# A gated delta rule on one core: where the decays' projection and the triangles' products stand among the values' convolutions

## The chip, the cores and the metric

The kernel runs on one core of a Trainium2 chip. The metric is device time in microseconds (us) of one execution, given as the median of the runs shown. The program is one decoder layer, in 32-bit floats throughout; the change touches its first part, the delta-rule attention, and nothing else.

The engines are TensorE (PE in the profile; its weight loads are PEld), VectorE (DVE), ScalarE (ACT), GpSimd (POOL) and SyncE (SP, which issues transfers). Each works through a queue of its own in order.

## What is computed

The part that the change touches, cut to what matters (batch B = 4, T = 1024 tokens, H = 4 heads, keys of 64, values of 128):

```python
normed = (x - mu) * rsqrt(var + EPS) * ln_w + ln_b
q = causal_conv_silu(normed @ Wq, conv_q)      # four taps along the tokens
k = causal_conv_silu(normed @ Wk, conv_k)
v = causal_conv_silu(normed @ Wv, conv_v)
beta = sigmoid(normed @ Wb)
g = -exp(A_log) * softplus(normed @ Wa + dt_bias)
# q, k made unit length per head; then, token by token:
S = S * exp(g_t)
v_eff = (v_t - k_t @ S) * beta_t
S = S + outer(k_t, v_eff)
o_t = q_t @ S
# o normalised, gated with silu(normed @ Wg), projected with Wo, added to x; layernorm
```

After it come a cross attention, a mixture of experts and layernorms, which the change leaves alone.

## The kernel before

**Slabs.** The 1024 tokens are cut into NS = 8 slabs of 128 tokens, all four batches at once. The token-by-token recurrence is computed slab by slab in a block form: inside a slab the decays are summed with triangular matrices of ones, a triangular matrix per batch and head is inverted, and the state S is carried from slab to slab.

**Generators and rounds.** The work is written as Python generators, and `interleave` runs them in turns: in each round every generator advances to its next `yield`. What a generator writes between two yields is called a stage here. The turn decides the written order. A scheduler then fixes each engine's order when the program is built, with the written order as priority; the order seen in the trace is close to the written one, but not always the same.

**The loop.** For slab i there are two interleaves. The first one runs

- `prepares(i+1)`: two chains of `prepare`, each for two batches. Stages: a product on POOL (L494), the matmul `pe` (L500) with its Exp on ACT (L502) and a product on POOL (L504), then the matmuls `pk` (L514), then eight products on DVE in all per pair of batches that write `bp` (L525).
- `inverts(i)`: two `invert`s. Stages: transposes `pw` (L587) and their copies, matmuls `pl` of 32x32 (L597), `pu` (L613, L620) with copies into `tr` and `tt` (L623, L625), `pl` of 64x64 (L629), which reads `tr`, then `pu` of 64x64 (L634) with a copy (L636).
- one chain of `decays(i+2)`, `values(i)` and `cumulated(i+2)`, in this order.

`decays` has three stages of TensorE work: the transposes `pt` of each half of the normalised input (L335), each followed by an ACT copy into `nT` (L339), and then the projection `pb` (L352): eight matmuls with eight columns each, which read both copies. Behind it stand some twenty operations on 128x16 elements, nearly all on DVE, that make `beta` and `g` (L365 to L388).

`values` runs `convolve` for four chunks c and two halves j: eight stages. Each holds two matmuls (L287, four records in the trace, since a 32-bit matmul leaves two); after the yield come one ACT copy with a scale (L297) and three DVE multiply-adds (L299).

`cumulated` multiplies `g` with the triangular matrices `le`, `gt` and with `ones` (`pd`, L397), yields, and takes the Exp of the result on ACT (`ex`, L407); four DVE operations turn it into `el` and `qw` (L413 to L417).

Behind this interleave, `silus(i)` applies Silu to the four value tiles (L485). Each is told to be issued after all Exps collected in `exps`, that of `cumulated` among them, so that ACT's function table is changed once.

The second interleave runs `scans(i)` (the recurrence and the output; its first stage transposes keys and queries, `ptok` L647, and the values, `pv` L650; `qk` L653 is made of `ptok` and `qw`), `blocks(i+1)`, `project(i+2)` (the convolutions of keys and queries, by the same `convolve`) and `normed(i+3)`.

With no `i+2` (slabs 6 and 7) the chain is `values` alone. `decays(0)` and `decays(1)` run ahead of the loop, beside `normed(1)` and beside `cumulated(0)` and `project(0)`.

**Banks.** All these matmuls take their output from seven PSUM banks of one tag in turn.

Of the kernel before, what the change touches and what calls it, by code (L numbers as in the profile page):

```python
# [110 lines left out]
def kernel(ctx: ExitStack, tc: tile.TileContext, a: dict, out: bass.AP):  # L111
# [3 lines left out]
    def bc(ap, shape):  # L115
        return ap.to_broadcast(shape)
# [5 lines left out]
    def bank(name, tag="bank", bufs=None):  # L122
        kw = {} if bufs is None else {"bufs": bufs}
        return ps_pool[0].tile([P, 512], F32, tag=tag, name=name, **kw)
# [96 lines left out]
    def interleave(*gens):  # L221

        gens = list(gens)
        while gens:
            for g in list(gens):
                if next(g, gens) is gens:
                    gens.remove(g)
# [53 lines left out]
    def convolve(dst, c, nT):  # L281

        w0 = C_CONV + c * KCONV
        for j in range(2):
            pp = bank("pp")
            for kc in range(KC):
                mm(  # L287
                    pp[:, 0 : 2 * (HALO + P)],
                    lhsT=wqkv[:, kc, c * P : (c + 1) * P],
                    rhs=nT[:, kc, 2 * j : 2 * j + 2, :].rearrange("p b t -> p (b t)"),  # L290
                    start=kc == 0,
                    stop=kc == KC - 1,
                )
            yield
            pre = pp[:, 0 : 2 * (HALO + P)].rearrange("p (b t) -> p b t", b=2)
            ch = dst[:, 2 * j : 2 * j + 2, :]
            nc.scalar.activation(ch, pre[:, :, 0:P], AF.Identity, scale=cols[:, w0 : w0 + 1])  # L297
            for n in range(1, KCONV):
                nc.vector.scalar_tensor_tensor(  # L299
                    ch, pre[:, :, n : n + P], cols[:, w0 + n : w0 + n + 1], ch, ALU.mult, ALU.add  # L300
                )
# [21 lines left out]
    def decays(i, made):  # L323

        nrm = made["nrm"]
        nT = slab.tile([P, KC, B, HALO + P], F32, tag="nT", name="nT")
        if i:
            nc.gpsimd.tensor_copy(nT[:, :, :, 0:HALO], before[-1][:, :, :, P:])
        else:
            nc.gpsimd.memset(nT[:, :, :, 0:HALO], 0.0)  # L330
        before.append(nT)
        for c in range(KC):
            pt = bank("pt")
            for b in range(B):
                nc.tensor.transpose(  # L335
                    pt[:, b * P : (b + 1) * P], nrm[b][:, c * P : (c + 1) * P], ident
                )
            yield
            nc.scalar.activation(  # L339
                nT[:, c, :, HALO:],  # L340
                pt.rearrange("p (b t) -> p b t", b=B),
                AF.Identity,
                scale=cols[:, C_LNW + c : C_LNW + c + 1],
                bias=cols[:, C_LNB + c : C_LNB + c + 1],
            )


        pb = bank("pb")
        pba = pb[:, 0 : B * 2 * H].rearrange("p (b n) -> p b n", b=B)
        for b in range(B):  # L350
            for kc in range(KC):
                mm(  # L352
                    pba[:, b, :],
                    lhsT=nT[:, kc, b, HALO:],
                    rhs=wba[:, kc, :],
                    start=kc == 0,
                    stop=kc == KC - 1,
                )
        yield

        def small(name):
            return slab.tile([P, B, H], F32, tag=name, name=name)

        beta, za, u, s, s2, p, g = (small(n) for n in ("beta", "za", "u", "s", "s2", "p", "g"))
        nc.scalar.activation(beta, pba[:, :, 0:H], AF.Exp, scale=-1.0)  # L365
        nc.vector.tensor_tensor(
            za,
            pba[:, :, H : 2 * H],
            bc(rows[:, R_DT : R_DT + H].unsqueeze(1), [P, B, H]),
            ALU.add,  # L370
        )
        nc.vector.tensor_scalar_add(beta, beta, 1.0)
        nc.vector.reciprocal(beta, beta)

        nc.vector.scalar_tensor_tensor(u, za, -1.0, za, ALU.mult, ALU.max)
        nc.scalar.activation(u, u, AF.Exp, scale=-1.0)
        nc.vector.tensor_scalar_add(s, u, 2.0)
        nc.vector.reciprocal(s, s)
        nc.vector.tensor_tensor(s, s, u, ALU.mult)
        nc.vector.tensor_tensor(s2, s, s, ALU.mult)  # L380
        nc.vector.tensor_scalar_mul(p, s2, 1.0 / 17)
        for k in (15, 13, 11, 9, 7, 5, 3):
            nc.vector.scalar_tensor_tensor(p, p, 1.0 / k, s2, ALU.add, ALU.mult)
        nc.vector.scalar_tensor_tensor(p, p, 1.0, s, ALU.add, ALU.mult)
        nc.vector.tensor_scalar_max(za, za, 0.0)
        nc.vector.scalar_tensor_tensor(g, p, 2.0, za, ALU.mult, ALU.add)
        nc.vector.tensor_tensor(g, g, bc(nega.unsqueeze(1), [P, B, H]), ALU.mult)
        nc.vector.tensor_scalar_max(g, g, -1e30)  # L388

        made.update(nT=nT, g=g, beta=beta)  # L390
# [83 lines left out]
    def values(made):  # L474
        made["v"] = v = [slab.tile([P, B, P], F32, tag=f"v{c}", name="v", bufs=1) for c in range(H)]
        for c in range(H):
            yield from convolve(v[c], NQK + c, made["nT"])
    def silus(made):

        with ExitStack() as behind:  # L480
            for e in exps:
                behind.enter_context(tc.issue_after(e.ins))
            exps.clear()
            for v in made["v"]:
                nc.scalar.activation(v, v, AF.Silu)  # L485
# [4 lines left out]
    def prepare(i, b, made):  # L490

        g, kq = made["g"], made["kq"]
        ee = work("ee", [P, H, 2, P])
        nc.gpsimd.tensor_tensor(  # L494
            ee[:, :, 1, :], bc(le.unsqueeze(1), [P, H, P]), bc(g[:, b, :].unsqueeze(2), [P, H, P]), ALU.mult
        )
        yield

        pe = bank("pe")
        mm(pe, lhsT=gt, rhs=ee[:, :, 1, :], start=True, stop=True)  # L500
        exps.append(
            nc.scalar.activation(ee[:, :, 0, :], pe.rearrange("p (h t) -> p h t", h=H), AF.Exp)  # L502
        )
        nc.gpsimd.tensor_tensor(  # L504
            ee[:, :, 1, :], ee[:, :, 0, :], bc(nge.unsqueeze(1), [P, H, P]), ALU.mult
        )
        yield

        bp = made["bp"]
        pks = [bank("pk") for par in range(2)]  # L510
        for r in range(2):
            for par, pk in enumerate(pks):
                h0 = slice(par * HK, (par + 1) * HK)
                mm(  # L514
                    pk[:, r * 2 * P : (r + 1) * 2 * P],
                    lhsT=kq[r][h0, 0, b, :],
                    rhs=kq[r][h0, :, b, :],
                    start=True,
                    stop=True,
                )  # L520
        yield
        for par, pk in enumerate(pks):
            for r in range(2):
                h = 2 * r + par
                nc.vector.scalar_tensor_tensor(  # L525
                    bp[:, :, b * H + h],
                    pk[:, r * 2 * P : (r + 1) * 2 * P].rearrange("p (n t) -> p n t", n=2),
                    made["nb"][:, b, h : h + 1],
                    ee[:, h],
                    ALU.mult,  # L530
                    ALU.mult,
                )
# [268 lines left out]
    made = [{} for _ in range(NS)]  # L801
# [6 lines left out]
    def prepares(i):  # L808
        made[i]["bp"] = slab.tile([P, 2, B * H, P], F32, tag="bp", name="bp", bufs=2)
        made[i]["tt"] = tts[i % 2]  # L810
        gens = [prepare(i, b, made[i]) for b in range(B)]
        return [chain(*gens[n::2]) for n in range(2)]

    def inverts(i):
        return [invert(b, made[i]) for b in range(0, B, 2)]

    def scans(i):
        return [
            chain(scan(i, b, made[i]), scan(i, b + 1, made[i])) for b in range(0, B, 2)
        ]  # L820
# [4 lines left out]
    def some(f, i, *args):  # L825
        return [f(*args, made[i])] if i < NS else []
# [5 lines left out]
    interleave(blocks(0, made[0]), *some(project, 1, 1))  # L832
    for i in range(NS):
        ahead = prepares(i + 1) if i + 1 < NS else []
        interleave(
            *ahead,
            *inverts(i),
            chain(*some(decays, i + 2, i + 2), values(made[i]), *some(cumulated, i + 2)),
        )
        silus(made[i])  # L840
        if i + 1 < NS:
            interleave(
                *scans(i), *some(blocks, i + 1, i + 1), *some(project, i + 2, i + 2), *some(normed, i + 3, i + 3)
            )
# [816 lines left out]
```

## Time and profile before

| what | us |
|---|---|
| median of three runs (1768.39, 1771.73, 1775.53) | 1771.73 |
| the profiled execution, device time | 1777.84 |
| its span, first to last instruction | 1776.1 |
| PE busy / DVE busy / ACT busy / POOL busy in the span | 1589.0 / 1177.7 / 935.8 / 565.8 |
| mean granted TensorE clock | 0.945 |

The delta rule takes some 800 us of the span. A slab begins with its transposes `pw`; these start at 108.5, 200.4, 290.9, 384.7, 476.8, 568.9, 659.6 and 737.1 us, so a slab takes these times (each window is one slab):

| slab | us | PE busy | DVE busy | ACT busy |
|---|---|---|---|---|
| 0 | 91.9 | 87.41 | 66.36 | 50.60 |
| 1 | 90.5 | 84.77 | 70.10 | 51.93 |
| 2 | 93.8 | 86.95 | 69.27 | 51.84 |
| 3 | 92.1 | 85.97 | 69.28 | 51.87 |
| 4 | 92.1 | 86.08 | 69.21 | 51.89 |
| 5 | 90.7 | 86.05 | 67.98 | 49.98 |
| 6 | 77.5 | 70.96 | 51.80 | 39.17 |

How to read the lines below: in the timeline each line has start and length in us, the engine, the line of the kernel, the operation, output and inputs, shape and number; a bracket tells how long the engine was idle before it and what ended the idle time. In the table of windows each pair is busy time and number of instructions, and PEclk is the granted clock as a share of full speed.

### The profile page before, as it was taken

How to read it: one execution, taken by the hardware profiler on the slowest of the kernel's cores; microseconds unless marked ns; L12 is line 12 of the kernel's file. 1: busy time of each engine (PE TensorE's matmuls, PEld its weight loads, DVE VectorE, ACT ScalarE, POOL GpSimd, SP SyncE). 2: the span in 40 equal slices, each digit the busy share in tenths (PEclk: the TensorE clock that was granted, in tenths of full speed). 3: DMA queues.
4: the chain of work that ended last, by engine and by line, in shares of the span. 5: the costliest groups of instructions: out<-in, count | busy, mean ns of one | idle time of the engine just before them, and what ended most of it. 6: DMA issues, size and time to landing. Idle time of an engine off the chain costs nothing. (4 is left out here: it accounts for less than half of the span.)

```text
span 1776.1 us, 28454 instructions
## 1 busy us (share of the span) xinstructions
PE 1589.0 (89%) x9524; PEld 1152.4 (65%) x9524; DVE 1177.7 (66%) x3557; ACT 935.8 (53%) x2214; POOL 565.8 (32%) x486
## 2 busy tenths in 40 slices
PE   4658999999989998985889999999989999999991
PEld 3246777676767766762657777887765666666660
DVE  4658686877777776735456888888865655555554
ACT  3425555555556454551278888888743333333333
POOL 2311312121212112014045666666733322222222
PEclk9869999898989898998999999999999999999995
DMA  4010101010101010103050011111263322332226
GB/s 142 18 19 22 39 19 43 19 43 19 43 19 30 19 31 19 25 31 132 0 190 13 22 46 43 37 49 37 94 216 67 69 45 46 46 48 46 45 33 199
DMA packets 119023, 94.20 MB, mean 53 GB/s; under 512 B 56939, under 2 KB 108639, under 8 KB 118367
## 3 DMA queue, kind: packets, MB, share of 16 engines
q1 hardware_dynamic: 100127, 69.14, 13.6%
q0 software_dynamic: 13296, 17.83, 6.0%
q10 hardware_dynamic: 5456, 5.41, 0.9%
q8 instruction: 78, 1.28, 0.3%
q14 instruction: 66, 0.54, 0.1%
HBM read 55.46 MB, written 36.90 MB: 52 GB/s over the span
## 5 line engine op out<-in xcount | busy, mean ns | idle before, releaser
L1536 POOL DMA_INDIRECT xd<-my,mrow x71 | 110.6, 1557 | 294.4 <-ACT my L1535 268.7
L1105 ACT ACTIVATE sc<-sc,ntop,rq 128x77 f32<-128x77 f32 x512 | 182.4, 448 | 5.2 <-DVE ntop L1100 4.6
L1136 PE MATMUL pxo<-ball,aT 128*128 128x256 f32 (+1 forms) x640 | 151.4, 384 | 0.8 <-DVE xs L1147 0.8
L287 PE MATMUL pp<-nT,wqkv 128*128 128x262 f32 x512 | 149.1, 430 | 0.2 <-PE pu L620 0.2
L1066 POOL TENSOR_TENSOR rq<-rq,nhalf 128x8 f32<-128x8 f32 x64 | 106.8, 1669 | 129.2 <-DVE rq L1065 128.1
L1487 PE MATMUL pgt<-wall,mxT 128*128 x284 | 134.6, 596 | 0.5 <-ACT mxT L1420 0.5
L1487 PE MATMUL pup<-wall,mxT 128*128 x284 | 134.4, 596 | 0.0
L1514 PE MATMUL pdn<-wdn,mhT 128*128 x568 | 134.2, 379 | 0.0
L759 POOL TENSOR_TENSOR so<-so,nhalf 128x4 f32<-128x4 f32 x32 | 32.6, 1018 | 312.3 <-DVE so L758 312.3
L1136 PEld LDWEIGHTS pxo<-ball,aT 128*128 128x128 f32 (+1 forms) x640 | 118.0, 192 | 15.1 <-DVE xs L1147 1.4
L1049 PE MATMUL pq<-wdn,xT 128*128 128x512 f32 x256 | 120.6, 594 | 1.5 <-ACT qsq L1059 1.0
L299 DVE SCALAR_TENSOR_TENSOR kq<-pp,cols,kq 128x256 f32<-128x256 f32 x192 | 88.3, 478 | 38.9 <-ACT kq L297 36.3
L287 PEld LDWEIGHTS pp<-nT,wqkv 128*128 128x128 f32 x512 | 99.6, 209 | 21.8 <-issue 3.3
L1514 PEld LDWEIGHTS pdn<-wdn,mhT 128*128 128x128 f32 x568 | 102.5, 190 | 11.0
L1495 DVE TENSOR_TENSOR sge<-pgt,ball 128x512 f32<-128x512 f32 x71 | 49.1, 692 | 85.3 <-PE pgt L1487 84.4
L1496 ACT ACTIVATE sge<-sge 128x512 f32<-128x512 f32 x71 | 44.7, 630 | 111.8 <-DVE sge L1495 111.8
L1487 PEld LDWEIGHTS pup<-wall,mxT 128*128 128x128 f32 x284 | 54.5, 192 | 69.0 <-issue 69.0
L1497 DVE TENSOR_TENSOR pup<-pup,ball 128x512 f32<-128x512 f32 x71 | 49.7, 699 | 69.8 <-PE pup L1487 69.7
L1114 POOL TENSOR_TENSOR sc<-sc,den 128x616 f32<-128x616 f32 x64 | 78.2, 1221 | 55.0 <-DVE den L1113 41.0
L1535 ACT ACTIVATE my<-my,mw 128x256 f32<-128x256 f32 x71 | 36.1, 508 | 106.3 <-DVE my L1534 106.3
L299 DVE SCALAR_TENSOR_TENSOR v<-pp,cols,v 128x256 f32<-128x256 f32 x192 | 81.6, 476 | 13.9 <-ACT v L297 13.2
L1085 PE MATMUL psc<-wdn,qT 128*128 128x154 f32 x512 | 78.7, 295 | 7.2 <-ACT qT L1077 7.2
(313 smaller groups left out, 3693.9 us busy)
## 6 DMA issues: line engine op xcount, KB each, us to landing
mx<-xg SPq DMA_DIRECT2D x71, 130.0 KB, 2.1
xs<-xd SPq DMA_DIRECT2D x12, 512.0 KB, 9.5
xi<-in_x SPq DMA_DIRECT2D x8, 512.0 KB, 5.1
am<-ab SPq DMA_DIRECT2D x16, 256.0 KB, 3.7
xd<-kd SPq DMA_DIRECT2D x32, 128.0 KB, 1.7
wall<-in_L_ffn_gate_w SPq DMA_DIRECT2D x8, 512.0 KB, 9.6
wall<-in_L_ffn_up_w SPq DMA_DIRECT2D x8, 512.0 KB, 8.6
xd<-xs SPq DMA_DIRECT2D x8, 512.0 KB, 4.8
```

The lines of the kernel that those rows point to most:

```text
L287: mm(pp[:, 0 : 2 * (HALO + P)], lhsT=wqkv[:, kc, c * P : (c + 1) * P], rhs=nT[:, kc, 2 * j : 2 * j + 2, :].rearrange("p b t -> p (b t)"), ...
L299: nc.vector.scalar_tensor_tensor(ch, pre[:, :, n : n + P], cols[:, w0 + n : w0 + n + 1], ch, ALU.mult, ALU.add)
L1049: mm(pq, lhsT=t["xT"][:, kc, :], rhs=xwq[:, kc, c0 : c0 + HH * XD], start=kc == 0, stop=kc == KC - 1,)
L1066: nc.gpsimd.tensor_tensor(rq, rq, nhalf[:, :HH], ALU.pow)
L1085: mm(ps[:, c * 2 * SC : (c + 1) * 2 * SC], lhsT=qT[:, 2 * g + c, :], rhs=kbd[:, b, half * XC // 2 + 2 * g + c, :], start=True, stop=True,)
L1105: nc.scalar.activation(sc[:, h], sc[:, h], AF.Exp, scale=t["rq"][:, h : h + 1], bias=t["ntop"][:, h : h + 1])
L1114: nc.gpsimd.tensor_tensor(sc, sc, bc(den.unsqueeze(2), [P, HH, SC]), ALU.mult)
L1136: mm(px[:, 0:D], lhsT=aT[:w, c, :], rhs=vo[:w, b, half * NV + c, :], start=half == 0 and c == 0, stop=half == 1 and c == NV - 1,)
L1487: mm(ps, lhsT=t["xT"][:, c, :], rhs=wall[:, bass.ds(e * EW + off + c * FF, FF)], start=c == 0, stop=c == KC - 1,)
L1497: nc.vector.tensor_tensor(pu, pu, ball[:, bass.ds(e * FF + B_U, FF)], ALU.add)
L1514: mm(px[:, 0:D], lhsT=t["hT"][:, f, :], rhs=wdn[:, bass.ds(e * EV + f * D, D)], start=f == 0, stop=f == FC - 1,)
L1536: nc.gpsimd.indirect_dma_start(out=xd, out_offset=bass.IndirectOffsetOnAxis(ap=row, axis=0), in_=y, in_offset=None, compute_op=ALU.add,)
```

## The change

Two edits. In `decays`, a `yield` is put between the second copy into `nT` and the projection `pb`, so that `pb`, the small operations behind it and all that follows in the chain move one round back. In the loop, the chain takes five stages of `values`, then `cumulated`, then the other three stages, instead of all eight and then `cumulated`. `islice(vals, 5)` stops right after the fifth yield: the matmuls of the fifth convolution are written, its copy and multiply-adds are written after `cumulated`.

```diff
@@ decays @@
                 bias=cols[:, C_LNB + c : C_LNB + c + 1],
             )
 
+        yield
 
         pb = bank("pb")
@@ the loop @@
     for i in range(NS):
         ahead = prepares(i + 1) if i + 1 < NS else []
+        vals = values(made[i])
         interleave(
             *ahead,
             *inverts(i),
-            chain(*some(decays, i + 2, i + 2), values(made[i]), *some(cumulated, i + 2)),
+            chain(*some(decays, i + 2, i + 2), islice(vals, 5), *some(cumulated, i + 2), vals),
         )
```

By rounds, the chain's TensorE work stands so, for slabs 0 to 5:

| round | before | after |
|---|---|---|
| 1, 2 | `pt` | `pt` |
| 3 | `pb` | nothing |
| 4 | convolution 0 | `pb` |
| 5 | 1 | convolution 0 |
| 6 to 9 | 2 to 5 | 1 to 4 |
| 10 | 6 | `pd` |
| 11 | 7 | convolution 5 |
| 12 | `pd` | 6 |
| 13 | | 7 |

The other generators of that interleave keep their rounds: `pl` of 64x64 stands in round 4, `pe` of the second pair of batches and `pu` of 64x64 in round 5, `pk` in round 6.

## The prediction

> **What bounds the kernel now.** I read the page's head first, then the windows of one slab, then the timeline around the changed lines in slabs 0 and 1.
>
> ```profile
> span 1776.1 us, 28454 instructions
> PE 1589.0 (89%) x9524; PEld 1152.4 (65%) x9524; DVE 1177.7 (66%) x3557; ACT 935.8 (53%) x2214; POOL 565.8 (32%) x486
> ```
>
> TensorE is busy in 89% of the span. But the change lives in a stretch of some 25 us in each slab, and there the mean says little. The windows of slab 1 (its `pw` starts at 200.4):
>
> ```profile
> 212.00:214.00 2.00, 1.61 (x27) 1.61 (x28) 1.75 (x8) 0.74 (x2) 1.27 (x2) 1.00 0.00 0
> 214.00:216.00 2.00, 2.00 (x12) 1.68 (x10) 0.91 (x5) 1.37 (x4) 0.78 (x1) 0.50 0.00 0
> 224.00:226.00 2.00, 2.00 (x9) 1.49 (x10) 2.00 (x8) 0.57 (x2) 0.00 (x0) 1.00 0.00 0
> 230.00:232.00 2.00, 0.77 (x6) 0.46 (x5) 2.00 (x6) 1.87 (x4) 0.00 (x0) 1.00 0.69 97
> 236.00:238.00 2.00, 1.46 (x12) 0.82 (x12) 1.96 (x4) 1.58 (x8) 0.00 (x0) 0.97 0.00 0
> ```
>
> The third pair is DVE. From 224 to 238 it is full, while PE (first pair) falls to 0.77 of 2 us at 230: the values' multiply-adds are DVE's backlog, and PE waits behind them. Later in the slab, from 250 on, PE is full. So two things count: when DVE's backlog ends, and what PE and ACT do until then.
>
> **Where the triangles' products hurt today.** Slab 0, end of the first interleave:
>
> ```profile
> 137.02 7.13 DVE L299 SCALAR_TENSOR_TENSOR v<-pp,cols,v 128x256 f32<-128x256 f32 x18
> 139.21 0.74 PE L397 MATMUL pd<-g,sq 128*128 128x16 f32 x6
> 139.98 0.21 ACT L407 ACTIVATE ex<-pd 128x48 f32<-128x48 f32 x1
> 140.21 1.28 ACT L485 ACT_TABLE_LOAD   x1
> 141.51 1.67 ACT L485 ACTIVATE v<-v 128x512 f32<-128x512 f32 x3
> 142.19 0.41 PE L650 MATMUL pv<-sq,v 128*128 128x128 f32 x1 [1.76 <-ACT v L485]
> 146.10 0.47 ACT L297 ACTIVATE kq<-pp,cols 128x256 f32<-128x256 f32 x1 [2.92 <-PE pp L287]
> 146.47 0.62 ACT L485 ACTIVATE v<-v 128x512 f32<-128x512 f32 x1
> ```
>
> `pd` comes behind all eight convolutions, the Exp behind `pd`, the table load behind the Exp, the first Silu behind the load: PE idles 1.76 us for it. The fourth value tile is complete on DVE at 144.15 (137.02 + 7.13), yet its Silu starts at 146.47: ahead of it in ACT's queue stands the copy of the next keys' convolution, whose matmuls on PE were late. The same tail in slab 1:
>
> ```profile
> 234.73 0.47 ACT L297 ACTIVATE kq<-pp,cols 128x256 f32<-128x256 f32 x1 [0.97 <-PE pp L287]
> 235.48 0.63 ACT L485 ACTIVATE v<-v 128x512 f32<-128x512 f32 x1 [0.27 <-DVE v L299]
> ```
>
> Here the key copy comes before DVE is done (235.44), and the last Silu follows at once. Reading the other slabs so: 0, 2, 3 and 4 lose 2.3 us between DVE's end and the last Silu, 1 and 5 lose 0.1 or less. And slabs 0, 2, 3, 4 last 91.9, 93.8, 92.1, 92.1 us, slabs 1 and 5 only 90.5 and 90.7.
>
> **Edit two, `pd` after five convolutions.** Nothing is added: six records of `pd` (0.74 us), one Exp (0.21), four DVE operations (235.36 to 235.95, 0.6 us). No transfer and no POOL work belongs to it; SP's and POOL's queues stay as they are.
> - Is `g` there? In slab 1 the last operation on `g` ends at 224.9. Convolutions 2 to 7 are 24 records in 5.57 us (slab 0), 0.23 each, so from 223.83 the twelve records of 2, 3 and 4 end at 226.6. `g` has 1.7 us to spare. Should PE wait in `pd`, convolutions 5 to 7 are behind it, and DVE waits for those: but ACT's last value copy ends at 230.1 and its multiply-adds begin at 234.0 (235.44 less three of 0.476), so 3.9 us of stall are covered.
> - The Exp then stands three convolutions earlier, 12 x 0.23 = 2.8 us. The load of 1.28 us and the first Silus fall between the value copies, where ACT now idles 0.41 us at a time; ACT's lead of 3.9 us takes the 1.28 + 2 x 0.62 = 2.5 us. [...]
> - Gain, first term: PE does `ptok`, `pv` and the key matmuls earlier, the key copy is ahead of DVE's end in every slab, and slabs 0, 2, 3 and 4 go as 1 and 5 do: 91.9 + 93.8 + 92.1 + 92.1 = 369.9, less 4 x 90.6 = 362.4, is **7.5 us**. The bounds are 0 (the orders stay) and 9.2 (4 x 2.3, the whole delay).
> - Gain, second term: the 1.76 us of idle PE goes in all six slabs. It is worth something only if PE moves work of its full part into it: one more round of key matmuls, 4 x 0.23 = 0.93 us, 5.6 in six slabs. If no bank is free it is worth 0. Between the two I take the middle, **2.8 us**, for banks are freed by DVE at one in 1.43 us just then.
> - The four small DVE operations move ahead of the last nine multiply-adds. DVE's sum is the same and `qk` behind them ends when it did: 0. If the last Silu sets the end instead, it is 0.6 later, 3.6 us in six slabs.
>
> **Edit one, the yield.** It removes and adds no instruction.
>
> ```profile
> 209.21 1.95 PE L352 MATMUL pb<-wba,nT 128*128 128x8 f32 x16
> 211.92 0.75 DVE L623 COPY tr<-pu 32x256 f32<-32x256 f32 x2
> 212.39 2.38 PE L629 MATMUL pl<-tr,bp 64*64 64x64 f32 x32 [1.23 <-DVE tr L623]
> 214.70 2.11 PE L287 MATMUL pp<-nT,wqkv 128*128 128x262 f32 x4
> 216.61 2.28 PE L500 MATMUL pe<-ee,sq 128*128 128x512 f32 x4
> ```
>
> `pb` starts at 209.21; its second copy ended at 208.4, so in the loop there is hardly a wait to remove. What stands next, `pl`, needs `tr`, which DVE copies only at 211.92, behind eight `bp` products. `pb` fills this hole. I take it that the order stays, as `pb` has its inputs 4 us before `pl` has: **0**. The other end is the first rival.
> - Convolution 0 goes behind `pe` and `pu`. PE's sum is equal. On DVE, three multiply-adds (1.43 us) come later, out of a stretch with gaps (0.91 of 2 us busy at 214); in return `pe` comes up to 2.1 us earlier, and with it eight `bp` products (3.2 us). I take **0**; the ends are 1.43 x 6 = 8.6 us lost and 2.1 x 6 = 12.6 gained, neither likely in full.
> - Ahead of the loop, `pb` of slab 1 moves behind one more key convolution (0.93 us) in a stretch where PE is full: 0, between -1 and +1.
>
> **The sum.** 7.5 + 2.8 = 10.3 us off. The profiled execution (1777.84, of which 1.7 outside its span) would become 1767.5; it is 6.1 above the median, and I apply the difference to the median: 1771.73 - 10.3 = **1761.4 us**. Its own range, with both gains at their ends and some loss on DVE, is 1756 to 1767.
>
> **Rivals.**
> - *`pb` lands behind `pl`* (slower). Then PE idles from 209.2 to 212.4, 3.2 us instead of 1.23, and `pb`'s 1.95 us follows `pl` uncovered: all behind it, DVE's backlog too, ends 1.95 later, 6 x 1.95 = 11.7. `g` comes later than convolution 4, so the first edit's gain goes too: **1783.4**. For it: the written order now says so. Against it: `pl` is not ready when PE is free. It decides as soon as the records of L352 follow those of L629. On the clock: after the 1.23 us gap the granted clock is already 0.50 at 214. [...]
> - *DVE gives it back* (no change). Convolution 0's multiply-adds all fall into the full stretch: +8.6, with the gain of 10.3: **1770.0**. For it: DVE is full from 224 to 238. Against it: the earlier `bp`.
> - *It doesn't do what it says* (no change). The decays' small operations, a round later, bring `g` after convolution 4; `pd` goes on behind the last convolution, and the Exp is as late as now: **1771.7**. For it: the 1.7 us to spare are less than the 1.95 of `pb`. Against it: without convolution 0 between them the small operations run closer together.
>
> **How the numbers follow.** Forecast 0.50, `pb` behind `pl` 0.28, DVE gives back 0.12, no effect 0.10. A measurement here tells about 0.5% (8.9 us) from no change: faster is below 1762.9, slower above 1780.6. Of the forecast four fifths lie below 1762.9: faster 0.40. The rest of it, 0.10, and the two cases without change give 0.32 for the same; slower 0.28. The range must reach to the slower case and take the larger gains: 1752 (both gains at their ends, 14.8, and a part of `pe`'s) to 1785.
>
> **What would show it.** Right: L352 still ahead of L629 on PE; `pd` between the value convolutions; the table load of L485 before the last value copy of L297; the 1.76 us before `pv` gone; the last Silu within 0.3 us of DVE's end in all slabs; slabs 0, 2, 3 and 4 at 90.6 or less. Wrong: L352 behind L629 with 3 us idle before it, an idle PE before `pd` released by `g`, or DVE's value products ending later in the slab than 35.0 to 37.6 us after its `pw`.

## The result, and the profile after

| kernel | median us | before, same chip | ratio to before, 95% interval |
|---|---|---|---|
| changed | 1796.86 | 1773.15 | 1.0128 [1.01, 1.0155] |

The change makes the kernel slower by 23.7 us, 1.3%. The forecast was 1761.4 in a range of 1752 to 1785: wrong in its sign, and the range misses by 12 us. The head of the page of the changed kernel:

```profile
span 1798.4 us, 28454 instructions
PE 1608.0 (89%) x9524; PEld 1167.0 (65%) x9524; DVE 1181.6 (66%) x3557; ACT 933.2 (52%) x2214; POOL 565.4 (31%) x486
```

The same instructions, a span 22.3 us longer, and 19 us more of busy TensorE: the matmuls themselves took longer. Slabs 0 to 5, from one first `pw` to the next, now take 94.5, 95.2, 96.0, 95.5, 95.9 and 93.4 us: 570.5 together, against 551.1 before. Slab 6, without these edits, adds 1.5 and the start 1.0.

The timeline of slab 1 (`pw` at 204.0) where the yield was put (lines past the yield are one higher now: L353 is `pb`, L624 the copy into `tr`, L630 the 64x64 `pl`):

```profile
215.62 0.75 DVE L624 COPY tr<-pu 32x256 f32<-32x256 f32 x2
216.18 3.64 PE L630 MATMUL pl<-tr,bp 64*64 64x64 f32 x32 [3.29 <-DVE tr L624]
219.75 3.58 PE L353 MATMUL pb<-wba,nT 128*128 128x8 f32 x16
223.18 3.76 PE L501 MATMUL pe<-ee,sq 128*128 128x512 f32 x4
226.87 3.67 PE L635 MATMUL pu<-tt,wt 64*64 64x64 f32 x32
230.48 2.11 PE L287 MATMUL pp<-nT,wqkv 128*128 128x262 f32 x4
232.52 3.67 PE L515 MATMUL pk<-kq 64*128 64x256 f32 x16
```

`pb` now stands behind `pl`. TensorE waits 3.29 us for `tr`, where it waited 1.23, and the same matmuls take half as long again or more: `pl` 3.64 instead of 2.38 us, `pb` 3.58 instead of 1.95, `pu` 3.67 instead of 2.07, `pk` 3.67 instead of 2.0. Why, the windows of the same slab show (window, length, then PE, PEld, DVE, ACT, POOL busy, then the granted clock):

```profile
214.00:216.00 2.00, 0.00 (x0) 0.00 (x0) 1.97 (x7) 0.00 (x0) 1.31 (x2) 0.87 0.00 0
216.00:218.00 2.00, 1.82 (x17) 1.85 (x18) 1.27 (x5) 0.36 (x1) 1.78 (x2) 0.50 0.03 8
222.00:224.00 2.00, 2.00 (x8) 1.66 (x8) 0.42 (x4) 0.63 (x2) 0.00 (x0) 0.50 0.00 0
228.00:230.00 2.00, 2.00 (x21) 2.00 (x21) 1.93 (x5) 1.04 (x3) 0.92 (x1) 0.50 0.00 0
234.00:236.00 2.00, 2.00 (x12) 1.33 (x8) 1.51 (x7) 0.00 (x0) 0.00 (x0) 0.51 0.00 0
236.00:238.00 2.00, 2.00 (x11) 1.63 (x10) 2.00 (x7) 0.47 (x1) 0.85 (x1) 1.00 0.00 0
```

The granted clock is 0.50 from 216 to 236, twenty microseconds. Before, it was 0.50 at 214 and back at 1.00 by 218, as the two windows of before that follow the prediction's row for 214 show:

```profile
216.00:218.00 2.00, 2.00 (x5) 1.07 (x5) 0.82 (x4) 0.96 (x2) 0.00 (x0) 0.65 0.00 0
218.00:220.00 2.00, 2.00 (x23) 1.24 (x22) 2.00 (x4) 1.94 (x4) 1.26 (x2) 1.00 0.00 0
```

With the change, VectorE (third pair) starves in that stretch: 0.42 of 2 us at 222.

The end of the first interleave in slab 0, whose lines of before the prediction showed:

```profile
144.38 0.74 PE L398 MATMUL pd<-g,sq 128*128 128x16 f32 x6
144.97 2.90 PE L287 MATMUL pp<-nT,wqkv 128*128 128x262 f32 x12
145.38 1.28 ACT L486 ACT_TABLE_LOAD   x1
146.68 0.63 ACT L486 ACTIVATE v<-v 128x512 f32<-128x512 f32 x1
146.79 5.31 DVE L299 SCALAR_TENSOR_TENSOR v<-pp,cols,v 128x256 f32<-128x256 f32 x13
148.14 0.27 PE L651 MATMUL pv<-sq,v 128*128 128x128 f32 x1
151.06 0.47 ACT L297 ACTIVATE kq<-pp,cols 128x256 f32<-128x256 f32 x1 [0.64 <-PE pp L287]
152.14 0.63 ACT L486 ACTIVATE v<-v 128x512 f32<-128x512 f32 x1 [0.60 <-DVE v L299]
```

Here the second edit did what was forecast: `pd` has three convolutions behind it, the table load stands among the value copies, `pv` no longer waits 1.76 us, the key copy is early and the last Silu follows VectorE's end (152.10) at once. But all of it comes late: VectorE's last value product ends 42.6 us after `pw`, instead of 35.6.

So each slab has a front that grew and a tail that shrank. For slabs 1 to 4, from `pw` to the end of VectorE's value products: 43.8 us on average (43.3 to 44.2) instead of 36.1 (35.1 to 37.6), 7.7 longer; from there to the next `pw`: 51.9 instead of 56.1, 4.2 shorter.

### The profile page after: what moved, and what is told of

Read it like the earlier page. It is cut to its first block, busy times and chain, and to the rows that moved or that the text cites. A ratio compares the mean times of both kernels' runs of the same rounds, so it can differ in the third digit from the quotient of the medians.

```text
span 1798.4 us, 28454 instructions
## 1 busy us (share of the span) xinstructions
PE 1608.0 (89%) x9524; PEld 1167.0 (65%) x9524; DVE 1181.6 (66%) x3557; ACT 933.2 (52%) x2214; POOL 565.4 (31%) x486
## 5 line engine op out<-in xcount | busy, mean ns | idle before, releaser
L287 PE MATMUL pp<-nT,wqkv 128*128 128x262 f32 x512 | 140.1, 412 | 0.3 <-PE pu L621 0.2
L1138 PEld LDWEIGHTS pxo<-ball,aT 128*128 128x128 f32 (+1 forms) x640 | 118.0, 192 | 15.1 <-DVE xs L1149 1.4
L287 PEld LDWEIGHTS pp<-nT,wqkv 128*128 128x128 f32 x512 | 95.5, 199 | 20.7 <-issue 3.1
L299 DVE SCALAR_TENSOR_TENSOR v<-pp,cols,v 128x256 f32<-128x256 f32 x192 | 81.2, 478 | 13.2 <-ACT v L297 12.5
```

What stands on the lines that cost most here:

```text
L287: mm(pp[:, 0 : 2 * (HALO + P)], lhsT=wqkv[:, kc, c * P : (c + 1) * P], rhs=nT[:, kc, 2 * j : 2 * j + 2, :].rearrange("p b t -> p (b t)"), ...
L299: nc.vector.scalar_tensor_tensor(ch, pre[:, :, n : n + P], cols[:, w0 + n : w0 + n + 1], ch, ALU.mult, ALU.add)
L1138: mm(px[:, 0:D], lhsT=aT[:w, c, :], rhs=vo[:w, b, half * NV + c, :], start=half == 0 and c == 0, stop=half == 1 and c == NV - 1,)
```

## The experiments

Ten kernels were run, each beside the kernel before. Theory A was formed from the trace above: the yield costs, by the order of `pb` and by the clock, and the second edit gains.

| kernel | median us | its before | ratio, 95% interval |
|---|---|---|---|
| second edit alone (`pd` behind five) | 1763.31 | 1774.89 | 0.9929 [0.9908, 0.9949] |
| first edit alone (the yield) | 1799.21 | 1774.89 | 1.0129 [1.0091, 1.0166] |
| both, the yield behind `pb` | 1763.37 | 1774.89 | 0.9927 [0.9896, 0.9958] |
| changed, wide filler | 1781.39 | 1774.89 | 1.0023 [1.0, 1.0046] |
| second edit alone, wide filler | 1762.49 | 1774.07 | 0.9929 [0.991, 0.9947] |
| changed, narrow filler | 1795.97 | 1774.07 | 1.0114 [1.0088, 1.0139] |
| `pd` behind three | 1774.31 | 1774.07 | 1.0004 [0.9988, 1.002] |
| `pd` behind four | 1774.99 | 1775.06 | 1.0002 [0.9988, 1.0016] |
| `pd` behind six | 1759.39 | 1775.06 | 0.9924 [0.99, 0.9947] |
| a convolution ahead of `pb` | 1767.20 | 1775.06 | 0.9963 [0.995, 0.9976] |

**The two edits apart.** The second edit alone, against the changed kernel, as are the edits below where nothing else is said:

```diff
-        yield
```

> The second edit alone: pd behind five convolutions, no yield in decays. Theory A (the yield costs, since pb no longer fills the hole ahead of the 64x64 pl and TensorE then runs at half clock for some 19 us instead of 8; the second edit gains): faster than before, 1758 to 1768 us, the 64x64 pl starting 12 us after its slab's pw as before, values' last multiply-add 35 to 37 us after it. Theory B (the loss comes from pd itself, which cuts the convolutions and puts the table load among the value copies): slower than before, 1780 us or more.

The first edit alone, here against the kernel before:

```diff
+        yield
 
         pb = bank("pb")
```

> The first edit alone: the yield in decays, pd behind all eight convolutions. Theory A: slower than the changed kernel, since the second edit's gain is missing too, 1797 to 1815 us; the hole before the 64x64 pl is 3.6 us and the granted clock 0.50 until about 31 us after pw. Theory B: near before, 1765 to 1780 us.

Theory A holds in both, theory B in neither: the second edit alone gains 11.6 us, the yield alone loses 24.3. Of theory A's clock, down until some 31 us after `pw` with the yield alone, slabs 0, 1 and 4 show it (30.5 to 32.2 us); in slabs 2, 3 and 5 it is back at 19.8 to 23.6 us. The tail of slab 3 with the second edit alone (`pw` at 379.7):

```profile
408.81 1.28 ACT L485 ACT_TABLE_LOAD   x1
411.56 0.27 PE L650 MATMUL pv<-sq,v 128*128 128x128 f32 x1
414.87 0.47 ACT L297 ACTIVATE kq<-pp,cols 128x256 f32<-128x256 f32 x1 [0.64 <-PE pp L287]
415.94 0.63 ACT L485 ACTIVATE v<-v 128x512 f32<-128x512 f32 x1 [0.60 <-DVE v L299]
```

No wait before the first `pv`, and the last Silu right behind VectorE (415.91), 36.2 us after `pw` instead of 38.2. Slabs 0 to 5 take 88.5, 89.2, 89.1, 88.4, 88.4 and 86.0 us. But it is not only this wait that counts. TensorE's waits from 26 to 50 us after `pw` (those above 0.25 us, added up) shrink only from 3.7 to 2.8 us a slab. The clock in the tail changes too; slab 3 from 40 to 44 us after `pw`, first of before, then of the second edit alone:

```profile
424.70:428.70 4.00, 3.12 (x16) 2.15 (x14) 2.16 (x10) 3.95 (x17) 0.00 (x0) 0.61 0.01 2
419.70:423.70 4.00, 4.00 (x33) 3.78 (x33) 1.28 (x6) 3.83 (x13) 0.00 (x0) 1.00 0.00 2
```

Before, every one of the six slabs spends 6.8 us of its tail (33 us after `pw` and later) at 0.50; with the second edit alone, only slab 1 does. Slab 1 gained 1.3 us, the other five 3.4 to 4.7.

Beside the yield, the second edit is worth little: 1796.9 with both and 1799.2 with the yield alone, intervals that overlap. This is not for want of a wait to remove. With the yield alone TensorE waits 1.76 us before the first `pv` in all six slabs, as in slab 1 (`pw` at 205.0):

```profile
245.19 0.33 PE L651 MATMUL pv<-sq,v 128*128 128x128 f32 x1 [1.76 <-ACT v L486]
```

With both edits 0.3 us or less is left of it, and from the end of VectorE's value products to the next `pw` a slab takes 52.1 us instead of 53.8. But those products end 43.0 us after `pw` instead of 41.6, on the average of six slabs: the clock, down in the same place, stays at 0.50 for 109 us in the six slabs from 8 to 33 us after `pw`, against 82 with the yield alone. Until `pd`, TensorE's order is the same in the two kernels; why the clock stays down longer was not found.

**The order of `pb`.** Both edits, but the yield behind `pb`'s own yield, so that all but `pb` is a round later:

```diff
-        yield
 
         pb = bank("pb")
...
+        yield
         yield
```

> Both edits, but the yield stands behind pb instead of ahead of it: pb fills the hole as before, the small operations and the convolutions stay a round back. Theory A (order of pb and clock): most of the loss is gone, 1765 to 1780 us; the hole is 1.7 us again. Rival C (what costs is that the first convolution and the small operations of the decays come a round later, which loads VectorE in its full stretch): little changes, 1788 us or more.

1763.37, a little below the 1765 to 1780 expected: the loss is gone, and rival C falls: that the first convolution and the small operations come a round later costs nothing that can be seen. Slab 3 of it (`pw` at 377.4):

```profile
386.23 1.95 PE L352 MATMUL pb<-wba,nT 128*128 128x8 f32 x16
389.45 2.32 PE L630 MATMUL pl<-tr,bp 64*64 64x64 f32 x32 [1.26 <-DVE tr L624]
391.70 3.37 PE L501 MATMUL pe<-ee,sq 128*128 128x512 f32 x4
```

`pb` fills the hole again and 1.26 us of it are left.

**How much of it is the clock.** The changed kernel with five throwaway matmuls where `pb` stood; their result is not used, nothing of the computation is left out:

```diff
+        if i >= 2:
+            fill = bank("fill")
+            for _ in range(5):
+                mm(
+                    fill[:, 0 : 3 * (HALO + P)],
+                    lhsT=ident,
+                    rhs=nT[:, 1, 0:3, :].rearrange("p b t -> p (b t)"),
+                    start=True,
+                    stop=True,
+                )
         yield
```

> The changed kernel with five throwaway matmuls of 393 columns (3.3 us at full clock, result not used) in the round where pb stood, so that TensorE stays busy with wide work until the 64x64 pl; everything else in the order of the changed kernel. Theory A with the clock as its larger part: the clock is 1.00 from pl on and the slab is 4 to 6 us shorter than the changed kernel's, 1762 to 1778 us, though work was added. Rival D (the late pb alone costs, by its 1.95 us and by the late decays; the clock follows and doesn't matter): 1793 to 1810 us.

Added work makes the changed kernel 15.5 us faster; in the ratios, 1.0023 against 1.0128. Its gain is short of the 1762 to 1778 expected, and one execution shows why. Two slabs of it, slab 1 (`pw` at 207.2) and slab 2 (at 299.9), windows as above:

```profile
221.00:225.00 4.00, 4.00 (x28) 3.42 (x27) 0.67 (x3) 3.32 (x7) 0.28 (x1) 0.71 0.00 0
225.00:229.00 4.00, 4.00 (x18) 1.98 (x16) 2.71 (x9) 1.30 (x3) 1.93 (x2) 0.50 0.00 0
229.00:233.00 4.00, 4.00 (x25) 3.21 (x24) 3.30 (x12) 0.00 (x0) 0.61 (x1) 0.50 0.00 0
...
313.70:317.70 4.00, 4.00 (x39) 3.45 (x38) 0.80 (x3) 2.89 (x6) 0.85 (x1) 1.00 0.02 4
317.70:321.70 4.00, 4.00 (x40) 2.77 (x41) 3.27 (x10) 1.63 (x6) 2.50 (x2) 1.00 0.00 0
```

In slab 1 the clock falls all the same, behind the filler, during `pb`; in slab 2 it stays at 1.00 in this stretch. Slabs 2, 3 and 5, where it stays up here or is down for some 3 us, take 272.1 us together; the changed kernel needs 284.9 for them and the second edit alone 263.5. So of the 7.1 us that the yield costs in each of these three slabs, 4.3 go with the clock (284.9 - 272.1 over three), and rival D falls. The other 2.9 (272.1 - 263.5 over three) belong to the late `pb`, but perhaps not all: with the filler the clock is down again for 3.4 to 6.8 us in the tail of these slabs, with the second edit alone it isn't. All this is one execution. In slabs 0, 1 and 4, where the clock fell again, the three together take 281.6 against 285.6: slab 0 is longer than without the filler (97.5 against 94.5), slab 4 is 4.6 shorter (91.3 against 95.9) with the clock down for 10 us instead of 20.

**Is it the length of the wait?** The changed kernel with a second, unused copy of `pb` in the round where `pb` stood:

```diff
+        if i >= 2:
+            fill = bank("fill")
+            for b in range(B):
+                for kc in range(KC):
+                    mm(
+                        fill[:, b * 2 * H : (b + 1) * 2 * H],
+                        lhsT=nT[:, kc, b, HALO:],
+                        rhs=wba[:, kc, :],
+                        start=kc == 0,
+                        stop=kc == KC - 1,
+                    )
         yield
```

> The changed kernel with a second copy of pb (eight matmuls of eight columns, result not used) in the round where pb stood: the hole before the 64x64 pl is filled as far as before, the real pb still comes behind pl. Theory E (the length of the idle time decides how long the clock stays down): as before, 8 us of half clock, 1772 to 1783 us. Theory F (what keeps the clock down is that narrow work, the 64x64 pl and pb, follows where wide work followed before; the idle time matters little): the clock stays at 0.50 until about 30 us after pw, 1790 to 1803 us.

1795.97: as slow as the changed kernel, though the wait is as short as before. Slab 3 (`pw` at 393.7), first the timeline of TensorE, then the windows:

```profile
402.54 1.95 PE L351 MATMUL fill<-wba,nT 128*128 128x8 f32 x16
405.69 3.67 PE L641 MATMUL pl<-tr,bp 64*64 64x64 f32 x32 [1.20 <-DVE tr L635]
409.29 3.58 PE L364 MATMUL pb<-wba,nT 128*128 128x8 f32 x16
412.73 3.76 PE L512 MATMUL pe<-ee,sq 128*128 128x512 f32 x4
```

```profile
403.00:407.00 4.00, 2.80 (x26) 2.71 (x26) 3.76 (x10) 0.36 (x1) 2.60 (x3) 0.77 0.01 4
407.00:411.00 4.00, 4.00 (x31) 3.88 (x30) 0.59 (x2) 1.52 (x3) 0.49 (x1) 0.50 0.00 0
419.00:423.00 4.00, 4.00 (x19) 2.92 (x19) 2.17 (x9) 0.47 (x1) 0.00 (x0) 0.50 0.02 4
```

A wait of 1.20 us, busy TensorE from then on, and a clock of 0.50 that still holds at 423. Theory E falls and F holds in slabs 0, 1, 3 and 4; in 2 and 5 the clock came back some 10 us earlier, as it did in slab 5 of the changed kernel. What differs from before is what follows the wait: there `pl` was followed by a convolution (262 columns) and `pe` (512 columns), here by `pb`, with eight columns a matmul.

In slab 0 of before (`pw` at 108.5) the clock fell with no wait ahead of it; TensorE is on 32x32 matmuls, then `pb`, then `pl`:

```profile
118.50:120.50 2.00, 2.00 (x52) 1.96 (x41) 1.97 (x6) 0.57 (x2) 1.19 (x2) 1.00 0.04 8
120.50:122.50 2.00, 2.00 (x28) 1.95 (x28) 1.55 (x7) 0.98 (x3) 0.89 (x1) 0.83 0.00 0
122.50:124.50 2.00, 2.00 (x13) 1.68 (x12) 0.67 (x3) 1.18 (x4) 0.00 (x0) 0.50 0.00 0
```

TensorE is busy throughout (2.00 of 2.00 us), and the clock falls to 0.50 at 121.8. So the 1.23 us wait of slab 1, after which the prediction saw the clock at 0.50, need not be the cause.

**Does a full clock help where nothing else is wrong?** The second edit alone, with three wide throwaway matmuls into unused columns of `pb`'s bank, behind `pb`:

```diff
+        if i >= 2:
+            for _ in range(3):
+                mm(
+                    pb[:, HK : HK + 3 * (HALO + P)],
+                    lhsT=ident,
+                    rhs=nT[:, 1, 0:3, :].rearrange("p b t -> p (b t)"),
+                    start=True,
+                    stop=True,
+                )
         yield
```

> The second edit alone (pb in its old place), with three throwaway matmuls of 393 columns (2.0 us at full clock, result not used) behind pb, in the hole that is left before the 64x64 pl. Theory A with the clock: the stretch of 0.5 to 0.7 granted clock from 12 to 20 us after pw goes or shrinks, each slab 1 to 2.5 us shorter than with the second edit alone, 1748 to 1758 us. Rival D (the clock follows the waits and costs nothing by itself): 1763 to 1770 us, the added work or nothing.

1762.49: no gain, between the two ranges expected and next to rival D's. Slab 3, first of the second edit alone, then with the filler, each from 12 us behind `pw` on:

```profile
391.70:395.70 4.00, 3.70 (x33) 3.55 (x34) 2.33 (x11) 1.67 (x4) 2.00 (x2) 0.61 0.02 4
395.70:399.70 4.00, 4.00 (x8) 2.02 (x6) 2.23 (x10) 2.06 (x6) 0.00 (x0) 0.54 0.00 0
```

```profile
391.50:395.50 4.00, 4.00 (x40) 3.17 (x39) 2.03 (x6) 2.32 (x6) 2.04 (x2) 1.00 0.00 0
395.50:399.50 4.00, 4.00 (x38) 2.67 (x38) 3.13 (x13) 3.24 (x8) 1.10 (x1) 1.00 0.00 0
```

The filler does keep the clock at 1.00 here (0.61 and 0.54 without it), but VectorE's value products end 35.8 us after `pw` with it and 36.2 without: it fits that this backlog sets the end of the stretch as long as TensorE is not far behind. Some 7 us at half clock seem to be covered here; the 20 of the changed kernel were not. This probe isn't clean: the filler also puts `pl` off by 0.5 to 2.3 us in five of the six slabs, so that a gain by the clock could be hidden by it.

**The place of `pd`.** The second edit alone, with another number in `islice`; three, four and six:

```diff
-            chain(*some(decays, i + 2, i + 2), islice(vals, 5), *some(cumulated, i + 2), vals),
+            chain(*some(decays, i + 2, i + 2), islice(vals, 6), *some(cumulated, i + 2), vals),
```

> The second edit alone with pd behind three of the eight stages. If an earlier Exp is what gains, as long as g is there: within 0.3% of the version with five, 1758 to 1768 us, or slower by up to 6 us where TensorE waits for g, which comes 25 us after pw while the third convolution's matmuls end at about 26.

> The second edit alone with pd behind four of the eight stages. If the place of the Exp is what counts, as with five, 1760 to 1768 us; if the order behind it decides, as it seemed with three, up to 1775 us.

> The second edit alone with pd behind six of the eight stages. If the place of the Exp is what counts, it gains a little less than with five, 1762 to 1770 us. If the gain with five is an accident of the order behind it (with three it was gone), it can fall anywhere up to 1775 us.

Six gains as five does (0.9924 and 0.9929), a little more than expected; three and four gain nothing, which was not expected of three and only half expected of four. With three, `pd` does not wait long for `g`, but the order behind it is another one; slab 3 (`pw` at 381.4):

```profile
407.27 1.28 ACT L485 ACT_TABLE_LOAD   x1
409.83 0.95 DVE L416 COPY qw<-ex 128x16 f32<-128x16 f32 x1
414.27 0.63 ACT L485 ACTIVATE v<-v 128x512 f32<-128x512 f32 x1 [2.14 <-DVE v L299]
414.39 0.63 PE L647 MATMUL ptok<-sq,kq 128*128 128x128 f32 x4 [1.66 <-DVE v L299]
```

The load is early, but a copy of 0.17 us takes 0.95 on VectorE, the second Silu comes at 32.9 us after `pw` (32.0 with five), and `ptok` waits 1.66 us for VectorE. Which of these takes the gain back was not tried, but the traces tell where it goes. TensorE's waits from 26 to 50 us after `pw` come to 3.3 to 3.9 us a slab with three and four (3.7 before, 1.8 to 3.0 with five and six): they stand in other places and are no shorter. And with three, slabs 0, 1 and 4 take 89.6, 89.4 and 89.7 us, with no half clock in the tail; slabs 2, 3 and 5 take 93.9, 92.1 and 91.2, with 10.2 us of it each.

**A useful matmul in the hole.** The values' first convolution is written ahead of `pb`, in its round, and the rest of the chain as with five; in `decays` the yield of the changed kernel stays, and `chained` steps over it. No result is left out:

```diff
+    def chained(i, vals):
+        if i + 2 < NS:
+            d = decays(i + 2, made[i + 2])
+            for _ in range(2):
+                next(d)
+                yield
+            next(d)
+            next(vals)
+            next(d)
+            yield
+            yield from d
+            yield from islice(vals, 4)
+            yield from cumulated(made[i + 2])
+        yield from vals
...
-            chain(*some(decays, i + 2, i + 2), islice(vals, 5), *some(cumulated, i + 2), vals),
+            chained(i, vals),
```

> The values' first convolution is put ahead of pb into the hole before the 64x64 pl: useful wide work where the filler stood, pb still ahead of pl; pd behind five convolutions. If VectorE's backlog is what sets the end of this stretch, its three multiply-adds (1.43 us) move into VectorE's idle time and each slab gains about that against the second edit alone: 1752 to 1760 us. If pb is put off far enough to make pl late (it takes a bank that frees at about 10.5 us after pw), the gain is used up: 1762 to 1772 us.

1767.20, slower than the second edit alone. The wait before `pl` shrinks to 0.78 us in slab 3 and `pl` is not late (12.5 us after `pw`), but `pb` begins 1.0 us later, `g` is complete at 27.2 us instead of 25.1, and VectorE's value products end at 37.1 instead of 36.2. The first convolution's multiply-adds did move into VectorE's idle time (15.1 to 16.7 us after `pw`), but VectorE then waits 2.16 us for `pu` ahead of the copy `tt`, where with the second edit alone it worked on `g`'s operations and waited 0.19. So the time is in the range named for the other case, but not by a late `pl`.

## Why the prediction was wrong

- *Edit two* was right, and nearly in size: 10.3 us forecast, 11.6 measured for it alone. The split was not, and the near match of the sum is in part luck. The first term had slabs 0, 2, 3 and 4 go as slabs 1 and 5 went; in fact all six gained, 1 and 5 too (89.2 and 86.0 instead of 90.5 and 90.7). The wait before `pv` is 1.76 us in four slabs, not in six; in slabs 1 and 5 it was 1.26. When it went, TensorE's waits in the tail became only some 1 us a slab shorter, and with them went the clock's 6.8 us at 0.50 in five of six tails, which no term of the sum held. That the clock makes up the rest fits the slabs (1.3 us gained where it stayed down, 3.4 to 4.7 where not), but no run took it by itself.
- *Edit one* is the step that failed: "I take it that the order stays, as `pb` has its inputs 4 us before `pl` has: 0". The order didn't stay: in the trace `pb` follows `pl`, which waits 3.29 us in slab 1, and the yield alone costs 24.3 us. TensorE's queue followed the written order, and `pb` stood behind an instruction that wasn't ready. That `pb` covers the hole had been read rightly from the trace; the price of taking the cover away belonged into the sum and not into a rival.
- *The first rival* named the mechanism, with its place: the wait was put at 3.2 us in slab 1 and is 3.29. Its price, 11.7 us, was half of the 23.7 measured. Against the second edit alone, whose gain the rival counted as lost too, the price was 22.0 us (11.7 + 10.3) and the measured loss is 33.6. The term that was missing is the clock: the price holds nothing for it. `pb` was priced at 1.95 us and takes 3.58, and in slab 1 everything from `pl` to `pk` runs at 0.50; the filler puts the clock at 4.3 of 7.1 us in each of three slabs.
- *The clock* was 0.50 at 214 in slab 1 of before, behind a wait of 1.23 us, and from that row it was right that it was lost already. How soon it came back was not asked: after 3.4 us there, after 20.5 us in slab 1 of the changed kernel. The length of the wait doesn't tell it here: in slab 3 the clock stays at 0.50 for 20.5 us behind a wait of 3.57 us (the changed kernel) and for 20.5 us behind one of 1.20 us (the narrow filler), and in slab 0 of before it fell with no wait.
- *The other rivals*: that the first convolution's products load VectorE was refuted by the yield behind `pb`; `g` does come later with the yield, but still ahead of `pd`.
- Open: in these executions the first slab starts between 107.8 and 112.9 us, which no edit explains; medians carry the verdicts, single slabs the mechanism.

## What to carry to other kernels

An instruction that seems to sit in the way of a queue may be the cover of a wait behind it: before it is moved, ask what the engine has at that place once it is gone. Price a moved matmul at the clock that the trace shows at its new place (`pb` took 1.95 us in slab 1 of before and 3.58 us behind `pl`), and ask how long the clock stays down there (3.4 us in that slab before, 20.5 us with the change), not only whether it falls. And a wait that goes is not yet a gain: the same edit takes 1.76 us of waiting out of most slabs alone and beside the yield, and is worth 11.6 us in the one case and next to nothing in the other.

The best kernels here are the second edit alone, with `pd` behind five or six of the stages (0.9929 and 0.9924), and both edits with the yield behind `pb` (0.9927), all faster than the kernel before and the changed one.

## What was not expected of the hardware

In slab 0 of before the granted clock fell from 1.00 (118.5 to 120.5) to 0.50 (from 122.5 on) with TensorE busy for 2.00 us of every 2.00. It also stayed at 0.50 with TensorE busy: in slab 3 with the narrow filler PE has 4.00 of 4.00 us at a clock of 0.50, from 407 to 411 and again from 419 to 423.

How long the clock is down is added up from windows of 2 us, from 8 to 33 us after `pw` in slabs 0 to 5; a window in which it changes shows a value between 0.50 and 1.00, such as 0.87 at 214 in slab 1 of the changed kernel. With `pb` of eight columns next behind the 64x64 `pl` it was down for 17.0 to 20.5 us in 12 of 18 slabs (the changed kernel, the yield alone, the narrow filler) and for 6.8 to 10.2 us in the other six. In four kernels with `pb` ahead of `pl` and a convolution (262 columns) or `pe` (512 columns) next behind it (before, the second edit alone, the yield behind `pb`, `pd` behind three) it was down for 3.4 to 10.2 us in 23 of 24 slabs and for 13.7 us in one. The two groups differ in most slabs and overlap in some, and the order alone does not decide: in slabs 1 and 5 of the changed kernel TensorE runs `pl`, `pb`, `pe` and `pu` in the same order, with 20.5 and 10.2 us at 0.50. What decides was not found.

With five wide matmuls ahead (the wide filler) the clock stayed at 1.00 in this stretch in slabs 2 and 5 and was down for 3.4 us in slab 3; in slabs 0, 1 and 4 it fell behind them, for 13.6, 13.7 and 10.2 us.
